# Wider groups and longer lags in the gather stage of a graph layer with experts

## The chip, the cores and the metric

The kernel runs on one core of one Trainium2 chip. The metric is device time in microseconds (us) of one execution. TensorE is written PE, VectorE DVE, ScalarE ACT, GpSimd POOL, SyncE SP; SP issues most of the direct DMAs, POOL issues the gathers.

## The reference, cut to what matters

`x` has 12500 nodes of 256 numbers. There are 212500 edges `src -> dst`, sorted by `dst`; every node has an edge to itself among them (a self-loop), which comes last among the edges of its node.

```python
h   = x * rsqrt(deg_out)[:, None]
m   = segment_sum(h[src], dst) * rsqrt(deg_in)[:, None]
y0  = m @ W_gc + b_gc + x @ W_res + b_res
y   = y0 + moe(y0)              # top 2 of 64 experts, 256 -> 512 -> 256
out = layernorm(x + batchnorm(y) * gamma + beta)
```

## The kernel before, in words

The kernel has five stages, one after another.

**Degrees** (L257 to L434). The out-degrees are counted with one-hot matrices in PE, and `r_out`, their inverse root, is made. In between, `columns` (L268) loads the edges of the head groups (below) and `windows` (L282) makes `n0`, the first node of each group's window.

**Scaled rows and the check** (L516 to L598). `x` lies in `acc` as 14 sets of columns. DVE (L533) and ACT (L531) scale them by `r_out`; SP stores each set to `h_d` in DRAM (L535). `Lanes.fetch` (L456) loads the edges of the lane groups, `src` and `dst`, into the tile `room`: pass 0 has 128 lanes, pass 1 has 54, of which the last is loaded by a DMA of its own (L467). `fitting` (L491) counts on DVE what does not fit in the windows; its steps are dealt out between the scalings (L538 to L541). Then `acc` is set to zero in 14 parts (L553, ten on POOL and four on DVE), each as soon as the store of that set has landed. A block under `If(unfit > 0)` (L557) is skipped when everything fits; no instruction moves across it.

**Gather rows** (L600 to L1119). A row is 128 edges: POOL gathers 128 rows of `h_d` by `src_col` into one of six `ring` buffers of four rows (L683), and PE multiplies them with a one-hot matrix `o` made by DVE (`one_hot`, L671), adding up a group of `GR = 8` rows in PSUM (L696). A group spans a window of `W = 128` nodes. There are `NG = 198` groups, so 1584 rows. The first `HG = 16` (head) groups take edges as they come. The other 182 take `L = 1078` edges each, of which `SKIP = 54` self-loops are left out and the remaining 1024 fill 8 rows; the self-loops are added from the window's own rows of `h_d` (`own`, L709, a DMA of SP; `add_own`, L738). To leave them out, `compact` (L990) runs 40 DVE steps over 1078 columns, once for the lanes of pass 0 and once for pass 1: compare, mark, a running count, then six rounds (`BITS`) of four operations that shift the kept edges together. `lay` (L1044), `lay_turn`, `laid` transpose the result into `src_col` and `rel`, and `marks` (L1074) takes a flag apart. The lanes lie in the last columns of `acc`, which are first saved to `lent_d` (L601) and later loaded back (L1108); the second `Lanes.fetch` (L603) loads them there, and its three memsets are on DVE (L462, L470).

After a group: `out_of` (ACT copy of PSUM, L730), `add_own` and `numbers` (DVE), `turn` (two PE transposes, L766), `to_nodes` (DVE adds into `acc` and into the in-degrees, L793). When all edges of a tile of 128 nodes are in, `nodes` (L816) works on a pair of tiles: in-degree root, `scale` of `x` (ACT), `turn_x` (PE), `dense` (PE, `y0` and the expert logits), `best` (DVE, top 2), `count` and `ranks` (position within each expert), `codes`, and for each tile and choice `entries` (DVE) and `enter` (PE), which write into `tab`, two tables in PSUM (tile number and lane) that say which node sits in which expert slot. `dense` to `best` and `count` to `ranks` take the two tiles of a pair one after the other, since `gp` and `pp` are in one PSUM bank.

The order is written out by hand (`tc.manual_schedule`, L1101): on PE, DVE, ACT and POOL each instruction of the stage comes in the order in which the program gives it. The loop (L1111) gives one `row(c)`, one `one_hot(c + AHEAD)`, and then those steps of the heap `todo` whose time, counted in rows, has come. A step gives its successor a time `lag` rows later (`later`, L641): 6 rows, falling to 1 towards the end. Instructions that stand outside that block, such as `Lanes.fetch`, are put by the compiler among them.

**End of the rows** (L1122 to L1182). `tab` is turned into a list of nodes (`slot`), and the experts are ordered by size.

**Experts and normalisation** (L1185 on). For each expert gather, two layers, scatter; then batch and layer norm.

Of the kernel before, what the change touches and what calls it, by code (L numbers as in the profile page):

```python
# [43 lines left out]
GR = 8  # L44
NG = 198
HG = 16
# [3 lines left out]
L = -(-(M - HE) // NL)  # L50
# [11 lines left out]
def center(g):  # L62
    return (241 * g) >> 2 if g < HG else CEN + ((2029 * (g - HG)) >> 5)

# [35 lines left out]
def gnn_moe_kernel(  # L100
# [26 lines left out]
    lent_d = dram.tile([P, 5 * L + 2 * ((L + 2) // 2)], F32, name="lent_d")  # L127
# [114 lines left out]
    n0_lane = edge.tile([P, 2], F32)  # L242
# [4 lines left out]
    with ExitStack() as stack:  # L247
# [20 lines left out]
        def columns():  # L268
            g = tables.rearrange("p a b c -> p (a b c)")[:, : 2 * P].rearrange(
                "p (k c) -> p k c", c=P  # L270
            )
            for k, e in enumerate((src, dst)):
                nc.sync.dma_start(g[:, k], e[:HE].rearrange("(p c) -> p c", c=P))
            f = two.tile([P, 4, P], F32, name="col_f")
            S.copy(f[:, :2], g)
            p = ps2.tile([P, 4, P], F32, name="col_p")
            for k in range(2):
                T.transpose(p[:, k], f[:, k], ident)
            S.copy(src_col[:, :HC], p[:, 0])
            S.copy(rel[:, :HC], p[:, 1])  # L280

        def windows():  # L282
# [10 lines left out]
            GP.iota(cen[:, :HG], pattern=[[241, HG]], base=0, channel_multiplier=0)  # L293
            GP.iota(cen[:, HG:], pattern=[[2029, NL]], base=CEN << 5, channel_multiplier=0)
            V.tensor_single_scalar(cen[:, :HG], cen[:, :HG], 2, op=ALU.arith_shift_right)
# [27 lines left out]
            for k, (lim_of, op) in enumerate(((0.0, ALU.is_lt), (float(W), ALU.is_ge))):  # L323
                V.tensor_scalar(
                    junk[:, k], rel[:, :HC], lim_of, None, op0=op, op1=ALU.add,
                    accum_out=bad[:, k : k + 1],
                )
# [110 lines left out]
    count = [P, NL - P]  # L438
    HALF = (L + 2) // 2
    ROOM = 5 * L + 2 * HALF  # L440

    class Lanes:
        def __init__(self, room):
            self.given = [
                [room[:, (2 * k + i) * L : (2 * k + i + 1) * L].bitcast(I32) for i in range(2)]
                for k in range(2)
            ]
            self.buf = room[:, 4 * L : 5 * L]

            self.left = room[:, 5 * L : 5 * L + HALF].bitcast(BF16)[:, : L + 1]  # L450
            self.at = room[:, 5 * L + HALF :].bitcast(BF16)[:, :L]
            self.is_self, self.again = (
                self.buf.bitcast(BF16)[:, i * L : (i + 1) * L] for i in range(2)
            )

        def fetch(self):  # L456
            for k in range(2):
                for i, e in enumerate((src, dst)):
                    t = self.given[k][i]
                    n = count[k] - k  # L460
                    if k:
                        V.memset(t, (0, BEHIND)[i])  # L462
                    a = HE + k * P * L
                    b = a + n * L
                    nc.sync.dma_start(t[:n], e[a:b].rearrange("(p c) -> p c", c=L))
                    if k:
                        nc.sync.dma_start(  # L467
                            t[n : n + 1, : M - b], e[b:].rearrange("(p c) -> p c", p=1)
                        )
            V.memset(self.left, 0.0)  # L470

        def leave_out(self, k, n_left):

            r = count[k]
            s, d = (t[:r] for t in self.given[k])
# [10 lines left out]
                    self.at[:r], d, n0_lane[:r, k : k + 1], 255.0,  # L486
# [4 lines left out]
    def fitting(lanes, k, n_left):  # L491

        r = count[k]

        def outside(i, lim_of, op):
            V.tensor_scalar(
                lanes.is_self[:r], lanes.at[:r], lim_of, None, op0=op, op1=ALU.add,
                accum_out=bad[:r, 2 + 2 * k + i : 3 + 2 * k + i],
            )

        def begins():
            junk = lanes.buf[:r, :r]
            V.scalar_tensor_tensor(
                junk, n0_b[:r, 0, HG + k * P : HG + k * P + r], 1.0, ident[:r, :r],
                op0=ALU.mult, op1=ALU.mult, accum_out=n0_lane[:r, k : k + 1],
            )

        return [begins] + lanes.leave_out(k, n_left) + [
# [3 lines left out]
                bad[:r, 6 + k : 7 + k], n_left[:r], SKIP - 0.5, op=ALU.is_lt  # L512
# [3 lines left out]
    with ExitStack() as stack:  # L516
# [5 lines left out]
        n_left = one.tile([P, 2], F32, name="n_left")  # L522
        steps_of = []
        for k in range(2):
            steps_of += fitting(lanes, k, n_left[:, k : k + 1])
        for i, (t0, n) in enumerate(GROUPS + [(NT - 1, 1)]):
# [11 lines left out]
            if i > 1:  # L538
                for f in steps_of[:2]:
                    f()  # L540
                del steps_of[:2]  # L541
        for f in steps_of:
# [63 lines left out]
    with ExitStack() as stack:  # L606
# [5 lines left out]
        hp = inner.enter_context(tc.tile_pool(name="s_hot", bufs=3))  # L612
# [11 lines left out]
        zero = one.tile([P, 2 * D], F32)  # L624
# [5 lines left out]
        tab = [ps1.tile([P, NSLOT], F32, name=f"tab{k}") for k in range(2)]  # L630

        bank = ps1.tile([P, 4 * P], F32, name="bank")
        gp = bank[:, :DL]
        pp = bank[:, DL : DL + 2 * E].rearrange("p (k e) -> p k e", e=E)
# [3 lines left out]
        LAG = 6  # L638
        todo = []

        def later(t, f, k=1):  # L641
            lag = min(LAG, max(1, LAG + (NC - 100 - t) // 10))
# [24 lines left out]

        o_of, o_last, row_last = {}, {}, {}
        p_of, s_of = {}, {}

        def one_hot(c):  # L671
            g, j = divmod(c, GR)
            if j == 0:
                o_of[g] = hp.tile([P, GR, W], F32, name="o")
            o_last[g] = V.tensor_scalar(  # L675
                o_of[g][:, j], lane, rel[:, c : c + 1], None, op0=ALU.is_equal
            )

        def row(c):
# [16 lines left out]
            i = T.matmul(p_of[g], o_of[g][:, j], r[:, k], start=j == 0, stop=j == GR - 1)  # L696
            if j == 0:
                sync(i, o_last.pop(g))
            if k == RR - 1:
                row_last[u] = i  # L700
            if j == GR - 1:
                del o_of[g]
                later(c, lambda t: out_of(g, t))

        spare = tables.rearrange("p a b c -> p (a b c)").bitcast(F32)
# [3 lines left out]
        def own(g):  # L709
# [3 lines left out]
            if g % 4 == 0:  # L713
                n = min(4, NG - g)
# [8 lines left out]
            nc.sync.dma_start(own_of[g], h_d[bass.ds(own_begins["n0"][g % 4], W)])  # L723


        def out_of(g, t):
# [8 lines left out]
            else:  # L735
                later(t, lambda t: turn(g, s, None, t))

        def add_own(g, s, t):  # L738
# [5 lines left out]
            if g % 2 == 0:  # L744
                later(t, lambda t: turn(g, s, None, t))

        def numbers(g, s, t):
            add_own(g, s, t)
            shift = two.tile([P, 2, P], F32, name="shift")
# [11 lines left out]
            later(t, lambda t: turn(g, s, (shift, e), t))  # L761
# [16 lines left out]
        def to_nodes(g, q, t):  # L778
# [15 lines left out]
            if g % 2 == 0:  # L794
                return
            k = first_node(g - 1) // P
            V.tensor_add(deg_in[:, k : k + TD], q[:, 2 * P : 2 * P + TD], deg_in[:, k : k + TD])
            ready = first_node(g + 1) // P if g < NG - 1 else NT
            while begun[0] < NT:
# [3 lines left out]
                nodes(begun[0], n, t)  # L803
                begun[0] += n

        xts = {}

        def fetch(t0):
# [3 lines left out]
            xts[t0] = two.tile([P, 2, D], F32, name="xt")  # L812
# [3 lines left out]
        def nodes(t0, n, t):  # L816
# [28 lines left out]
            def scale(t):  # L845
                for i in range(n):
                    S.activation(xt[:r, i], xt[:r, i], AF.Copy, scale=v["root"][:r, i : i + 1])
                later(t, turn_x)
# [11 lines left out]
            def turned(t):  # L860
                q = v.pop("q").rearrange("p (i k n) -> p i k n", i=2, k=2)
                S.copy(of("xT", [P, 2, 2, P])[:, :n, :, :r], q[:, :n, :, :r])
                of("y", [P, 2, DL])
                of("top", [P, 2, 8])
                of("i8", [P, 2, 8], U32)
                take("gp", t, lambda t: dense(0, t))

            def dense(i, t):
                a = (t0 + i) * P
                for k in range(2):  # L870
                    T.matmul(gp[:r], acc2[:, k, a : a + r], wcat[:, k], start=k == 0, stop=False)  # L871
                for k in range(2):
                    T.matmul(  # L873
                        gp[:r], v["xT"][:, i, k, :r], wcat[:, 2 + k], start=False, stop=k == 1
                    )
                later(t, lambda t: best(i, t))

            def best(i, t):
                y, top, i8 = v["y"], v["top"], v["i8"]
                V.scalar_tensor_tensor(  # L880
                    y[:r, i], gp[:r], r_in[:r, t0 + i : t0 + i + 1], bias[:r],
                    op0=ALU.mult, op1=ALU.add,
                )
                V.max(top[:r, i], y[:r, i, D:])
                V.max_index(i8[:r, i], top[:r, i], y[:r, i, D:])
                if i < n - 1:
                    later(t, lambda t: dense(i + 1, t))
                    return
                give("gp", t)
                nc.sync.dma_start(  # L890
# [18 lines left out]
                take("pp", t, lambda t: count(0, t))  # L909
# [8 lines left out]
            def count(i, t):  # L918
                both = v["both"]
                T.matmul(pp[:r, 0], before[:r, :r], both[:r, i], start=True, stop=True)  # L920
                T.matmul(pp[:, 1], ones_b[:r], both[:r, i], start=True, stop=True)  # L921
                later(t, lambda t: ranks(i, t))

            def ranks(i, t):
                ahead = of("ahead", [P, E])
# [583 lines left out]
```

## Time and profile before

| what | us |
|---|---|
| median of 10 runs (lowest, highest) | 3413.92 (3411.93, 3418.39) |
| the profiled execution | 3413.97 |
| its span, first to last instruction | 3412.0 |
| `r_out` ready, first lane load issued | 196.65 |
| first gather of the rows starts | 258.64 |
| last gather of the rows starts | 2286.88 |
| first gather of the experts starts | 2325.45 |

| engine | busy us | share |
|---|---|---|
| PE | 2662.3 | 78% |
| DVE | 1753.8 | 51% |
| ACT | 748.3 | 22% |
| POOL | 2035.4 | 60% |

Times in the trace are counted from the first instruction. The profile names instructions by line, engine, operation and tiles; "SPq" is the queue of DMAs that SP issues. A wait is put down to what ended it; "issue" is time in which nothing that the profile shows was waited for.

### The profile page before, as it was taken

To read this page: it belongs to the slowest core of one execution; us is meant where nothing else is said; L and a number is where in the kernel's file an instruction comes from. 1 tells how busy PE (TensorE), PEld (TensorE's weight loads), DVE (VectorE), ACT (ScalarE), POOL (GpSimd) and SP (SyncE) were. 2 spreads that over 40 slices of the span, in tenths; PEclk is the share of its full clock that TensorE was granted. 3 is DMA by queue.
4 is the path that set the end of the run, shared out by engine and by line. 5 is a ranking of instruction groups with operands and counts; after the bars stand their busy time and mean duration, and the time that the engine had idled before them with its cause. 6 is when DMAs were issued, how large, how long until landed. Compare 5 with 4: busy or idle time off the path is not lost. (4 is left out here: it accounts for less than half of the span.)

```text
span 3412.0 us, 38328 instructions
## 1 busy us (share of the span) xinstructions
PE 2662.3 (78%) x11391; PEld 1774.1 (52%) x11391; DVE 1753.8 (51%) x6362; ACT 748.3 (22%) x2080; POOL 2035.4 (60%) x2086
## 2 busy tenths in 40 slices
PE   6723777777777777778777877877999999999644
PEld 5613444444444444444444444554778766778533
DVE  9977354855555555555555555574222221222498
ACT  8840010111111111111111111111222211222368
POOL 0017777777777777777777777764555555554100
PEclk8766888788988888988989889988999999999765
DMA  5058744354444444444444444434344445556667
GB/s 173 2 172 299 260 130 125 112 168 128 131 128 131 132 131 131 130 130 129 129 131 130 129 133 131 130 116 124 118 124 134 126 152 163 177 182 197 221 214 239
DMA packets 264826, 506.70 MB, mean 149 GB/s; under 512 B 45451, under 2 KB 177977, under 8 KB 256166
## 3 DMA queue, kind: packets, MB, share of 16 engines
q0 software_dynamic: 98800, 264.95, 26.7%
q1 hardware_dynamic: 152516, 226.44, 20.2%
q10 hardware_dynamic: 13298, 12.80, 1.3%
q8 instruction: 93, 1.52, 0.2%
q14 instruction: 119, 0.97, 0.1%
HBM read 411.01 MB, written 96.44 MB: 149 GB/s over the span
## 5 line engine op out<-in xcount | busy, mean ns | idle before, releaser
L683 POOL DMA_INDIRECT ring<-h_d,src_col x1584 | 1546.9, 977 | 494.2 <-issue 421.6
L696 PE MATMUL p<-ring,o 128*128 128x258 f32 x3168 | 1141.8, 466 | 485.0 <-DMA ring<-h_d,src_col 367.1
L696 PEld LDWEIGHTS p<-ring,o 128*128 128x128 f32 x3168 | 571.2, 212 | 950.0 <-DMA ring<-h_d,src_col 693.6
L675 DVE TENSOR_SCALAR o<-lane,rel 128x128 f32<-128x128 f32 x1584 | 394.4, 298 | 167.3 <-PE p L696 167.2
L1249 PE MATMUL yp<-w,h 128*128 128x256 f32 (+3 forms) x1928 | 432.9, 380 | 0.0
L1205 POOL DMA_INDIRECT xg<-x_d,tables x241 | 232.9, 967 | 317.8 <-PE xtp L1220 219.0
L730 ACT COPY s<-p 128x258 f32<-128x258 f32 x198 | 74.0, 374 | 1511.1 <-PE p L696 1489.8
L1233 PE MATMUL hp<-xT,w 128*128 128x384 f32 (+11 forms) x1328 | 399.2, 454 | 1.4 <-DVE xT L1224 1.4
L1249 PEld LDWEIGHTS yp<-w,h 128*128 128x128 f32 (+3 forms) x1928 | 341.8, 182 | 64.5 <-issue 7.3
L1237 ACT ACTIVATE h<-hp,w 128x384 f32<-128x384 f32 (+11 forms) x332 | 180.9, 545 | 669.8 <-PE hp L1233 669.3
L1233 PEld LDWEIGHTS hp<-xT,w 128*128 128x128 f32 x1328 | 248.4, 191 | 131.1 <-issue 56.7
L1255 POOL DMA_INDIRECT z_d<-yo,tables x241 | 238.1, 988 | 121.9 <-DVE yo L1254 65.3
L1224 DVE COPY xT<-xtp 128x768 f32<-128x768 f32 (+2 forms) x83 | 77.3, 932 | 405.1 <-PE xtp L1220 405.1
L880 DVE SCALAR_TENSOR_TENSOR y<-bank,r_in,bias 128x320 f32<-128x320 f32 x98 | 53.9, 550 | 378.0 <-PE bank L921 271.5
L1254 DVE TENSOR_TENSOR yo<-yp,bb 128x256 f32<-128x256 f32 (+3 forms) x241 | 102.0, 423 | 276.4 <-PE yp L1249 272.4
L793 DVE TENSOR_TENSOR acc<-q,acc 128x256 f32 x198 | 83.1, 420 | 226.9 <-PE q L770 114.3
L405 ACT ACTIVATE s_lo<-lane_b,nb 128x128 bf16<-128x128 bf16 x581 | 170.8, 390 | 3.7 <-DVE lo_end L396 2.5
L871 PE MATMUL bank<-wcat,acc 128*128 128x320 f32 x392 | 157.3, 535 | 1.3 <-DVE total L927 0.7
L553 POOL MEMSET acc<- 128x1792 f32 x10 | 15.9, 1591 | 228.6 <-DMA h_d<-acc 227.8
L982 PE MATMUL tab<-at,vals 128*128 128x512 bf16 x392 | 124.2, 402 | 10.3 <-DVE vals L971 10.2
L873 PE MATMUL bank<-wcat,xT 128*128 128x320 f32 x392 | 132.1, 462 | 0.0
L871 PEld LDWEIGHTS bank<-wcat,acc 128*128 128x128 f32 x392 | 96.0, 246 | 37.0 <-issue 14.7
(279 smaller groups left out, 2744.5 us busy)
## 6 DMA issues: line engine op xcount, KB each, us to landing
w<-in_wpack SPq DMA_DIRECT2D x64, 1026.0 KB, 5.3
ring<-h_d,src_col POOLq DMA_INDIRECT x1584
z_d<-zero SPq DMA_DIRECT2D x98, 256.0 KB, 5.2
zt<-z_d SPq DMA_DIRECT2D x24, 1024.0 KB, 7.1
tables<-h_d SPq DMA_DIRECT2D x182, 128.0 KB, 2.3
xt<-in_x ACTq DMA_DIRECT2D x48, 256.0 KB, 3.1
x_d<-y SPq DMA_DIRECT2D x48, 256.0 KB, 2.4
z<-in_x SPq DMA_DIRECT2D x12, 1024.0 KB, 7.3
```

The costliest lines, as they stand in the source:

```text
L405: S.activation(s_lo[:, i], lane_b, AF.Sign, bias=nb[:, k, i : i + 1])
L675: o_last[g] = V.tensor_scalar(o_of[g][:, j], lane, rel[:, c : c + 1], None, op0=ALU.is_equal)
L683: i = GP.indirect_dma_start(out=r[:, k, :D], out_offset=None, in_=h_d, in_offset=bass.IndirectOffsetOnAxis(ap=src_col[:, c : c + 1], axis=0),)
L696: i = T.matmul(p_of[g], o_of[g][:, j], r[:, k], start=j == 0, stop=j == GR - 1)
L871: T.matmul(gp[:r], acc2[:, k, a : a + r], wcat[:, k], start=k == 0, stop=False)
L873: T.matmul(gp[:r], v["xT"][:, i, k, :r], wcat[:, 2 + k], start=False, stop=k == 1)
L982: T.matmul(tab[m], vals[:r, m], at[:r], start=t0 + i + k == 0, stop=t0 + i == NT - 1 and k == 1,)
L1205: GP.indirect_dma_start(out=g, out_offset=None, in_=x2_d, in_offset=bass.IndirectOffsetOnAxis(ap=at[:, 0, k : k + 1], axis=0),)
L1233: T.matmul(hp[:, :m], w1[:, c, j * P : (j + 1) * P], xT[:, c, :m], start=c == 0, stop=c == 1,)
L1237: S.activation(h1[:, j, :m], hp[:, :m], AF.Gelu, bias=w[:, 2 * H + 4 * D + j : 2 * H + 4 * D + j + 1],)
L1249: T.matmul(yp[:r], h1[:, j, k * P : k * P + r], w2[:, j], start=j == 0, stop=j == 3,)
L1255: st = GP.indirect_dma_start(out=z_d, out_offset=bass.IndirectOffsetOnAxis(ap=at[:r, 1, k : k + 1], axis=0), in_=yo[:r], in_offset=None, b ...
```

## The change

Groups have twelve rows, and there are 132 of them, so again 1584 rows. The head has 14 groups (168 rows). The other 118 fit in one pass of 118 lanes with `L = 1620` edges, of which 84 self-loops are left out; seven rounds in `compact`. The second pass is gone, two copies to float are added at its end in place of the ACT copies of `lay`. The steps of the pass are spread over the first 101 rows. `Lanes.fetch` sets all lanes to zero first, on POOL, and `fitting` comes after all scalings. The lag is 11 rows instead of 6. One-hot matrices come in units of six rows, five buffers, 16 rows ahead. `dense` to `best` and `count` to `ranks` take both tiles of a pair at once (a second PSUM bank); the two tables become one, in which both numbers are summed. A counter (`hold`) lets at most two transposes be under way. Where several units of tiles become ready at once, each starts six rows after the one before.

```diff
-GR = 8
-NG = 198
-HG = 16
+GR = 12
+NG = 132
+HG = 14
...
-L = -(-(M - HE) // NL)
+L = -(-(M - HE) // NL // 2) * 2
...
         def fetch(self):
-            for k in range(2):
-                for i, e in enumerate((src, dst)):
-                    t = self.given[k][i]
-                    n = count[k] - k
-                    if k:
-                        V.memset(t, (0, BEHIND)[i])
...
-            V.memset(self.left, 0.0)
+            b = HE + (NL - 1) * L
+            for i, e in enumerate((src, dst)):
+                t = self.given[i]
+                GP.memset(t, (0, BEHIND)[i])
+                nc.sync.dma_start(t[: NL - 1], e[HE:b].rearrange("(p c) -> p c", c=L))
+                nc.sync.dma_start(
+                    t[NL - 1 : NL, : M - b], e[b:].rearrange("(p c) -> p c", p=1)
+                )
+            GP.memset(self.left, 0.0)
...
-            if i > 1:
-                for f in steps_of[:2]:
-                    f()
-                del steps_of[:2]
-        for f in steps_of:
+        for f in fitting(lanes, n_left):
             f()
...
-        hp = inner.enter_context(tc.tile_pool(name="s_hot", bufs=3))
+        hp = inner.enter_context(tc.tile_pool(name="s_hot", bufs=5))
...
-        tab = [ps1.tile([P, NSLOT], F32, name=f"tab{k}") for k in range(2)]
-
-        bank = ps1.tile([P, 4 * P], F32, name="bank")
-        gp = bank[:, :DL]
-        pp = bank[:, DL : DL + 2 * E].rearrange("p (k e) -> p k e", e=E)
-        LAG = 6
+        tab = ps1.tile([P, NSLOT], F32, name="tab")
+        banks = [ps1.tile([P, 4 * P], F32, name=f"bank{i}") for i in range(2)]
+        gps = [b[:, :DL] for b in banks]
+        pps = [b[:, DL : DL + 2 * E].rearrange("p (k e) -> p k e", e=E) for b in banks]
+        LAG = 11
...
-            lag = min(LAG, max(1, LAG + (NC - 100 - t) // 10))
+            lag = min(LAG, max(1, (NC - 10 - t) // 12))
...
+        def hold(t, f):
+            to_turn.append(f)
+            next_turn(t)
+
+        def next_turn(t):
+            while to_turn and turning[0] < 2:
+                turning[0] += 1
+                to_turn.pop(0)(t)
...
             ready = first_node(g + 1) // P if g < NG - 1 else NT
+            wait = 0
             while begun[0] < NT:
                 n = 2 if begun[0] < NT - 2 else 1
                 if begun[0] + n > ready:
                     break
-                nodes(begun[0], n, t)
+                if wait:
+                    at_row(t + wait, lambda t, t0=begun[0], n=n: nodes(t0, n, t))
+                else:
+                    nodes(begun[0], n, t)
                 begun[0] += n
+                wait += 6
...
-                        tab[m], vals[:r, m], at[:r],
+                        tab, vals[:r, m], at[:r],
...
+                lambda: V.tensor_copy(before_[:, full], m[:, full]),
+                lambda: V.tensor_copy(f[:, full], b[:, full]),
...
-        def compact_from(k, c):
-
-            per = 1 if k else 0.5
-            steps_of = compact(k)
...
+        def compact_by(c):
+
+            steps_of = compact()
+            lays = [(j, which) for j in range(0, GR, 4) for which in range(2)]
+            c -= 3 * len(lays) + 3 * LAG
+            for i, f in enumerate(steps_of):
+                at_row(c * i / len(steps_of), lambda t, f=f: f())
...
-            AHEAD = GR + 2
+            AHEAD = 16
             fetch(0)
-            compact_from(0, 0)
-            c = compact_from(1, 2 * P)
+            compact_by(HC - AHEAD)
...
-        V.scalar_tensor_tensor(node, node, float(P), tab[1], op0=ALU.mult, op1=ALU.add)
```

## The prediction

> **What bounds the kernel now.** I read the slices of the page first, then its costliest group, then the waits of POOL.
>
> ```profile
> PE   6723777777777777778777877877999999999644
> DVE  9977354855555555555555555574222221222498
> POOL 0017777777777777777777777764555555554100
> ...
> L683 POOL DMA_INDIRECT ring<-h_d,src_col x1584 | 1546.9, 977 | 494.2 <-issue 421.6
> ```
> ```profile
> POOL ring L683 <- issue: 421.6, 1384, 0.3
> ...
> POOL ring L683 <- PE p L696: 28.6, 94, 0.3
> ```
>
> POOL stands at 7 through the rows, and its gathers never wait: no idle time before one is longer than 0.4 us except the first. A gather takes 0.945 us undisturbed plus 0.30 between two: 1.25 us, and windows of 100 us hold 80 of them all the way. 1584 x 1.25 = 1980 us, but the rows last from 258.64 to 2287.83, that is 2029: some 50 us of gathers that are themselves longer. PE (78% busy) waits for the gathers, not they for it. So what can move the time is when the rows begin, what stretches a gather, and what follows the last one. Lag, units of one-hots, pairs at once and the counter of transposes change when PE, DVE and ACT do things that POOL does not wait for: nothing within the rows, with 24 ring rows (30 us) of cover; without it a late row costs its lateness. The row count stays 1584.
>
> **(a) Before the rows.** Windows of the DMAs between `r_out` and the first row:
>
> ```profile
> 201.00:206.00 5.00, 0.00 (x0) 0.00 (x0) 5.00 (x6) 5.00 (x13) 0.00 (x0) 0.50 0.08 30
> 206.00:213.00 7.00, 0.00 (x0) 0.00 (x0) 7.00 (x8) 4.16 (x11) 0.00 (x0) 0.50 0.91 306
> 213.00:220.00 7.00, 0.00 (x0) 0.00 (x0) 2.96 (x4) 0.00 (x0) 0.00 (x0) 0.50 0.07 26
> 221.00:252.00 31.00, 0.19 (x2) 0.11 (x2) 20.46 (x24) 0.00 (x0) 15.91 (x10) 0.50 1.01 341
> ```
>
> The last two columns are DMA share and GB/s. Twice the DMAs run at 26 GB/s, a sixteenth: one engine of 16, busy with the two 223 KB loads of 53 lanes. First SP sits 6.29 us in the load issued at 199.13; then a `fitting` step on DVE waits 4.8 us for such a load and the scalings behind it come late (SP waits 7.4 us for DVE). In between and after, the stores run at 341 GB/s. About 13 us are lost. After: no 53-lane load, and scalings ahead of all `fitting` steps. DVE then has 9 sets of 2.02 us done by about 215, faster than the stores take them; `fitting` (ten steps, some 12 us at 1620 columns) ends by 230, before the stores. Against it, the first load now waits for a POOL memset: 1.59 us for 1792 columns (L553), so 1.44 for 1620. The loads are 117 x 1620 x 4 B = 758 KB each. Is that shape fast? The 128-lane one (539 KB) landed in 4.8 us; by that row 6.8 us, by the 53-lane one 29 us on one engine. I take the 128-lane row, the nearer. **-12 us**, ends -14 and (one engine) +32. The Trainium skill ("DMA: Bandwidth & Descriptors", "Why a DMA increments its semaphore by 16 and not by 1") says that a DMA uses the largest number up to 16 that divides its outer sizes; that agrees with 53 on one engine, and would give 117 thirteen, leaving the sum as it is.
>
> **(b) Memsets in POOL's queue.** The second fetch, after the `If`, has three memsets on POOL that must wait until the copy to `lent_d` has read its columns; the gathers stand behind them. That copy was issued at 257.74 and DVE's memset got through at 268.85: 11.1 us. How many gathers the compiler puts ahead of the memsets is not in this trace, but SP's order is: three of the 98 zero stores came ahead of the loads that wait for the same copy, so I take four gathers (5 us). POOL then idles 11.1 - 0.9 - 5 = 5.2 us, and the memsets take 3 x 1.44 plus gaps: **+10 us**. Ends: 4.3 (nine gathers or more ahead), 14.5 (none). The first gather is seen 0.9 us after that copy's issue. The lanes then land about 20 us after the rows begin; 16 one-hots are made by then.
>
> **(c) What stretches gathers.** The order of DVE and POOL during pass 0:
>
> ```profile
> 284.68 2.40 DVE L998 TENSOR_TENSOR_SCAN acc<-acc 128x1078 f32<-128x1078 bf16 x1
> 285.00 2.84 POOL L683 DMA_INDIRECT ring<-h_d,src_col  x1 [0.30 <-issue]
> ...
> 296.31 1.27 DVE L1026 TENSOR_TENSOR acc<-acc 128x1078 int32<-128x1078 int32 x1
> 296.62 1.78 POOL L683 DMA_INDIRECT ring<-h_d,src_col  x1 [0.30 <-issue]
> 297.62 1.28 DVE L1027 TENSOR_TENSOR acc<-acc 128x1078 int32<-128x1078 int32 x1
> 298.70 1.01 POOL L683 DMA_INDIRECT ring<-h_d,src_col  x1 [0.30 <-issue]
> ```
>
> A gather that starts while DVE runs a long operation on two SBUF tiles goes on only at that operation's end and then takes 0.83 us: 297.58 + 0.83 = 298.41, seen 298.40. So do the others of this pass. An operation that begins more than 0.1 us after the gather does not hurt it, and the DVE operations themselves do not stretch (L1026: 1.261 to 1.275 us). Summed over 0.945 us, pass 0 costs 12 us and pass 1 14 us. They are that cheap because DVE is full: operations of 1.27 us, end to end, each catch at most one gather late in its run.
>
> After: 46 steps at 1620 columns, one per 2.2 rows. There are 29 two-input steps of 1.27 x 1620 / 1078 = 1.91 us. A gather starts somewhere in each; on average half a period (0.63) after its beginning, and 0.1 is free: 1.91 - 0.73 = 1.18 us, 34 us in all. The scan (2.40, so 3.6) gives 2.9. The 14 short ones (0.72, so 1.07 us, seen to hold a gather too) catch one only part of the time: 0.97 x 0.97 / 2.5 = 0.37 each, 5. Together 42 instead of 26: **+16 us**. Ends: 0 in all (-26), and 1.8 for each of the 29 (+34). DVE has room: 75 us of steps and 25 of one-hots in 101 rows, 126 us and more. If it had none, the layout at row 101 would be late; it is needed at row 152. The Trainium skill ("SBUF — State Buffer", "Who interferes with whom") says that DVE and POOL share one pair of ports and that whichever issues first blocks the other. As an estimate by that rule, were half of the collisions to fall on DVE, this part would cost 21 and the time would be 3420; in this trace the gather is the one that waits.
>
> **(d) Steady rows.** `add_own` (0.476 us, two SBUF tiles, x182) stretches gathers by 0.04 us on average in the windows I summed; 64 fewer: **-3 us**. `to_nodes` reads PSUM and stretched none. The phase to POOL's beat may change; at worst each of 118 loses 0.3 us more, +35, at best -8.
>
> **(e) After the last gather.** Its start is R, now 2286.88.
>
> ```profile
> 2286.88 0.95 POOL L683 DMA_INDIRECT ring<-h_d,src_col  x1 [0.30 <-issue]
> 2325.45 0.94 POOL L1205 DMA_INDIRECT xg<-x_d,tables  x1 [37.63 <-DVEq L1293]
> ```
>
> By `first_node` the last group now sets free tiles 96 and 97, both at once, step by step side by side; the pair 94 was under way before. After, with 95 nodes per group, it sets free 94+95, 96 and 97, six steps apart. At lag 1 that is an order in which `dense` of 96 stands on PE behind the last `enter` of 94, and `scales` of 97 on DVE behind `best` of 96. From the rows of this tail: gather to PE 2.8, matmul 0.7, copy, `numbers`, `turn`, `to_nodes` to R + 6.9 (now R + 11.3, behind pair 94). Pair 94: root and `scales` 1.7, `scale` to `xT` 2.6, `dense` 3.7 + 2.4 (first tile on a slow clock), `best` 3.1: R + 20.5. `scales` 96 1.2, `ranks` 2.0, `codes` 1.25, `entries` 4 x 0.65, to 27.5; PE's four `enter` of 0.95 end at 29.4. `dense` 96 2.5, `best` 2.0: 33.9. `scales` 97, `ranks`, `codes`, `entries`: 38.6; `enter` 39.8; `dense` 97 2.5, `best` 2.0: 44.3; `ranks` to `enter`: 49.3. Slot list 5.25, less 0.75 for the second table: 53.8; copies and first gather: R + 55.1. Now it is R + 38.6: **+16.5 us**. Ends: +8 (DVE's work of a pair, 12 us, less the 4.4 of the earlier start) and +20.
>
> The rest is covered: what `columns` adds is one short memset against smaller `windows`; 66 fewer own loads are SP's; ACT is 22% busy.
>
> **Sum.** -12 + 10 + 16 - 3 + 16.5 = +27.5. The profiled execution took 3413.97 (span 3412.0, 2.0 around it), 0.05 over the median of the runs. Forecast 3441.
>
> **Rivals.** *Gathers go free* (faster): with steps spread out, DVE comes upon a gather already under way and waits for it. For it: DVE is no longer full, and gathers fill 76% of POOL's time. Against it: DVE's unchanged durations. Waits of (c) at zero: 27.5 - 42 = -14.5, 3399; below 14 us of waits in all, it turns the sign. *Light*: memsets without idle (+5), tail at +9, (c) at 30: 3413 to 3420. *Heavy*: add_own and entries fall on POOL's beat: up to 3475. *One engine for 117 lanes*: two loads of 29 us in a row, +32 in (a) and about +30 at the second fetch: 3490 to 3505; against it, the shape is nearer to 128. *The change does not do what it says*: the slow path under `If`. Counted on the reference's own edges, no edge falls outside a window and the poorest lane has 87 self-loops for 84: left out.
>
> **Chances.** Forecast (3424 to 3456) 0.64, light 0.14, gathers free 0.10, heavy 0.07, one engine 0.05. A change of 0.2% is about what a measurement here can tell (3407.1 and 3420.7): light lies within it for 0.11. So faster 0.10, same 0.11, slower 0.79. The range 3414 to 3460 leaves out the free gathers, one engine and the edges of light and heavy.
>
> **What would show it.** (a) first gather near 246 and no 26 GB/s windows; (b) three POOL memsets among the first gathers, with idle time ahead; (c) gathers of 1.5 to 2.9 us spread over the first 100, none later; (e) R to the experts' first gather near 55 us. I am wrong if DVE's long steps stretch instead of gathers, or if the tail's units overlap.

## The result, and the profile after

| what | before | after |
|---|---|---|
| median of the runs shown with the result, us | 3414.43 (28 runs) | 3429.75 (8 runs, 3427.11 to 3431.81) |
| ratio | | 1.0044 [1.0035, 1.0052] |
| span of the profiled execution | 3412.0 | 3424.9 |
| first gather of the rows starts | 258.64 | 243.74 |
| last gather of the rows starts | 2286.88 | 2284.79 |
| first gather of the experts starts | 2325.45 | 2339.59 |
| gathers above 0.945 us, summed over all rows | 52.5 | 60.4 |

The changed kernel is slower by 0.4%. The profiled execution after took 3426.7 us, 3.0 below its median; the account below is of the spans, which differ by 12.9. The last row of the table, and every "excess" below, is added up from durations as the views print them, to 0.01 us; from the unrounded records it is 51.0 and 58.8, with nearly the same difference.

The page of the changed kernel: three lines of the slices, and its costliest group.

```profile
PE   6824777777777778777777777776999999999644
...
DVE  9976434454445445445454455664222222222498
...
POOL 0038777777777777777777777754555555554100
...
L693 POOL DMA_INDIRECT ring<-h_d,src_col x1584 | 1554.8, 982 | 495.2 <-issue 425.4
```

POOL's third slice reads 3 and read 1, its fourth 8 and 7: the rows now begin within the third (part of that 3 is memsets that have moved to POOL). The 1584 gathers (now L693) take 982 ns on average and took 977. The waits of POOL in front of them (sum, times, longest):

```profile
POOL ring L693 <- issue: 425.4, 1397, 0.3
...
POOL ring L693 <- PE p L707: 43.9, 144, 0.3
```

As before none of these is above 0.3 us: POOL sets the pace. In all the rows two gaps are longer than 0.4 us, one with the three memsets (below) and one of 1.2 us at row 140, which a DMA of the ring ended. Then the stretches between `r_out` (195.3) and the first row, with DMA share and GB/s last:

```profile
199.00:205.00 6.00, 0.00 (x0) 0.00 (x0) 6.00 (x5) 6.00 (x17) 0.77 (x1) 0.50 0.94 299
205.00:232.00 27.00, 0.19 (x2) 0.11 (x2) 19.66 (x21) 3.98 (x10) 15.93 (x10) 0.50 1.06 365
```

The DMA engines are nearly full from 199 to 232; nothing moves at 26 GB/s any more. At the second fetch, POOL's order of time:

```profile
272.80 0.94 POOL L693 DMA_INDIRECT ring<-h_d,src_col  x1 [0.30 <-issue]
273.73 2.86 POOL L461 MEMSET acc<- 128x1620 int32 x2
276.50 1.48 POOL L466 MEMSET acc<- 128x1621 bf16 x1
278.15 0.95 POOL L693 DMA_INDIRECT ring<-h_d,src_col  x1 [0.16 <-issue]
```

The three memsets stand behind 24 gathers. The gather after them would have begun at 274.05, so they cost 4.1 us, with no idle time ahead of them. The compaction, DVE beside POOL:

```profile
314.78 1.84 DVE L1051 TENSOR_TENSOR acc<-acc 118x1620 int32<-118x1620 int32 x1
314.90 2.54 POOL L693 DMA_INDIRECT ring<-h_d,src_col  x1 [0.30 <-issue]
...
316.54 0.67 DVE L685 TENSOR_SCALAR o<-lane,rel 128x128 f32<-128x128 f32 x3
317.12 1.84 DVE L1052 TENSOR_TENSOR acc<-acc 118x1620 int32<-118x1620 int32 x1
317.74 2.04 POOL L693 DMA_INDIRECT ring<-h_d,src_col  x1 [0.31 <-issue]
```

The step of 314.78 ends at 316.62; 0.83 us later, at 317.45, the gather that started on it is seen to end at 317.44. The same holds at 317.12: 318.96 + 0.83 = 319.79, seen 319.78. The DVE steps do not stretch (1.84 us each). Last, the end of the rows on POOL and PE:

```profile
2284.79 0.95 POOL L693 DMA_INDIRECT ring<-h_d,src_col  x1 [0.30 <-issue]
2339.59 0.94 POOL L1222 DMA_INDIRECT xg<-x_d,tables  x1 [53.85 <-DVE tables L1319]
```
```profile
2309.23 3.44 PE L1007 MATMUL tab<-at,vals 128*128 128x512 bf16 x8 [2.45 <-DVE vals L996]
2312.50 1.24 PE L893 MATMUL bank<-wcat,acc 128*128 128x320 f32 x4
...
2320.64 1.89 PE L1007 MATMUL tab<-at,vals 128*128 128x512 bf16 x4 [1.84 <-DVE vals L996]
2322.32 2.34 PE L893 MATMUL bank<-wcat,acc 128*84 128x320 f32 x4
```

L1007 is `enter`, L893 `dense`. `dense` of tile 96 (2312.50) comes right behind the last `enter` of pair 94, and `dense` of tile 97 (2322.32) right behind that of tile 96: the three units run one after the other. From the last row's gather to the first expert's it is 54.8 us, and was 38.6.

### The profile page after: what moved, and what is told of

It is laid out like the page before. It is cut to its first block, busy times and chain, and to the rows that moved or that the text cites. A ratio compares the mean times of both kernels' runs of the same rounds, so it can differ in the third digit from the quotient of the medians.

```text
span 3424.9 us, 37022 instructions
## 1 busy us (share of the span) xinstructions
PE 2663.8 (78%) x11121; PEld 1764.4 (52%) x11121; DVE 1635.7 (48%) x6013; ACT 707.8 (21%) x1994; POOL 2051.8 (60%) x2092
## 5 line engine op out<-in xcount | busy, mean ns | idle before, releaser
L693 POOL DMA_INDIRECT ring<-h_d,src_col x1584 | 1554.8, 982 | 495.2 <-issue 425.4
L707 PE MATMUL p<-ring,o 128*128 128x258 f32 x3168 | 1184.1, 484 | 506.8 <-DMA ring<-h_d,src_col 411.4
L707 PEld LDWEIGHTS p<-ring,o 128*128 128x128 f32 x3168 | 611.6, 224 | 998.5 <-DMA ring<-h_d,src_col 652.2
L685 DVE TENSOR_SCALAR o<-lane,rel 128x128 f32<-128x128 f32 x1584 | 375.5, 298 | 607.2 <-PE p L707 607.0
L742 ACT COPY s<-p 128x258 f32<-128x258 f32 x132 | 49.4, 374 | 1300.9 <-PE p L707 1298.5
L1007 PE MATMUL tab<-at,vals 128*128 128x512 bf16 x392 | 141.4, 451 | 11.3 <-DVE vals L996 11.3
L893 PE MATMUL bank<-wcat,acc 128*128 128x320 f32 x392 | 133.2, 466 | 0.0
L806 DVE TENSOR_TENSOR acc<-q,acc 128x256 f32 x132 | 55.6, 422 | 146.4 <-PE q L783 103.8
L898 PE MATMUL bank<-wcat,xT 128*128 128x320 f32 x392 | 123.9, 439 | 0.0
L702 ACT CAST ring<-mark 128x4 f32<-128x4 bf16 x354 | 57.8, 197 | 261.3 <-issue 261.2
L414 PE MATMUL deg_s<-o_hi,s_lo 128*128 128x98 bf16 x581 | 76.8, 232 | 27.5 <-DVE o_hi L202 18.3
```

The lines of the kernel that those rows point to most:

```text
L685: o_last[u] = V.tensor_scalar(o_of[u][:, j], lane, rel[:, c : c + 1], None, op0=ALU.is_equal)
L693: i = GP.indirect_dma_start(out=r[:, k, :D], out_offset=None, in_=h_d, in_offset=bass.IndirectOffsetOnAxis(ap=src_col[:, c : c + 1], axis=0),)
L707: i = T.matmul(p_of[g], o_of[v][:, n], r[:, k], start=j == 0, stop=j == GR - 1)
L893: T.matmul(gps[i][:r], acc2[:, k, a : a + r], wcat[:, k], start=k == 0, stop=False,)
L898: T.matmul(gps[i][:r], v["xT"][:, i, k, :r], wcat[:, 2 + k], start=False, stop=k == 1,)
L1007: T.matmul(tab, vals[:r, m], at[:r], start=t0 + i + k + m == 0, stop=t0 + i == NT - 1 and k + m == 2,)
```

## The experiments

They ran on other chips, three of them, which granted TensorE a lower clock: 0.787 over the changed kernel's span where the first chip gave 0.857. The kernel before took 3700 to 3706 us there. Times are compared only on the same chip, and the kernel before ran on each; for the rest the parts of the spans are compared. "Excess" is the sum of what gathers took above 0.945 us.

### The changed kernel on such a chip

> The changed kernel itself, as the measure for the others of this call on their chip. If this chip grants PE a clock of about 0.86, as in the profile after: ratio to the kernel before 1.0044 (1.0035 to 1.0052), excess of the gathers over 0.945 us in rows 0 to 95 45 us, in the others 15 us, 54.8 us from the start of the last row's gather to that of the first expert's. Where the clock is nearer to 0.79, PE sets the pace of the rows and what stretches gathers counts for less: ratio about 1.00, while excess and end of the rows stay what they are (within 3 us).

3714.96 us, ratio 1.0034 [1.0020, 1.0049]; excess 45.0 in rows 0 to 95 and 17.1 in the others; end of the rows 60.3. One line of the windows of each, first the changed kernel on the first chip, then here:

```profile
1200.00:1300.00 100.00, 76.28 (x253) 44.76 (x254) 46.51 (x222) 9.61 (x40) 75.93 (x80) 0.86 0.44 127
```
```profile
1200.00:1300.00 100.00, 65.62 (x218) 43.67 (x216) 39.40 (x195) 7.33 (x31) 66.34 (x70) 0.73 0.38 111
```

The third figure from the right is the granted clock. 80 gathers in 100 us became 70, and the waits of POOL say why:

```profile
POOL ring L693 <- issue: 437.1, 1424, 1.2
...
POOL ring L693 <- remote: 164.3, 61, 4.1
...
POOL ring L693 <- PE p L707: 102.9, 57, 8.5
```

Where the view says "remote", the profile names no instruction that ended the wait. But apart from the three memsets POOL stands still for more than 0.4 us in front of 107 gathers, and 104 of these are the first of a ring buffer: it waits for PE to free the ring, up to 8.5 us at a time, which it never did on the first chip. PE sets the pace. What stretches a gather is the same in both (45.0 us), but part of it is hidden behind PE; the end of the rows is longer, because PE lags behind the last gather: its last product of a row ends 10.2 us after that gather starts, and 5.1 on the first chip. The ratio near 1.00 that was expected for such a clock was too low: the end of the rows and the first rows still count.

### The compaction in pieces

```diff
+            def each(f, a=0, z=L):
+                k = 4
+                n = -(-(z - a) // k // 2) * 2
+                for x in range(a, z, n):
+                    out_steps.append(lambda x=x, y=min(x + n, z): f(x, y))
...
-                    lambda: V.tensor_tensor(b, w, m, op=ALU.bitwise_and),
+                each(lambda x, y: V.tensor_tensor(
+                    b[:, x:y], w[:, x:y], m[:, x:y], op=ALU.bitwise_and))
```

So for every step but the scan and a memset. A sum in `leave_out` (`n_left`) that nothing reads there is left out.

> The changed kernel with each step of the compaction (but the scan and one memset) cut into four pieces of about 405 columns. Theory (a gather that starts under a long two-input operation waits for that operation's end, so the price grows with the square of its length): the first 96 gathers lose some 12 us over 0.945 us each instead of 45, first to last gather about 2008 us, time about 3397. Rival (a price per operation, or per microsecond of DVE work): four times as many operations and as much work, so the gathers lose 45 us or more, time 3430 or above.

Excess in rows 0 to 95 24.7 us (45.0 in again, 45.7 in wait2); rows 152 on are unchanged. Time 3697.5, ratio 0.9984 [0.9973, 0.9995]. So the price is one of length and not of number, and the rival falls. But 24.7 is twice what was expected; the run `chain` shows why.

### The units of tiles closer together

```diff
-                wait += 6
+                wait += 2
```

> The changed kernel with the units of tiles that become ready together started two rows apart instead of six; that happens only after the last group. Theory (the order puts one unit's steps behind another's): last gather of the rows to first gather of the experts about 44 us instead of 54.8, time about 3419. Rival (the added pair of tiles costs its own work, whatever the order): 50 us or more, time 3425 or above.

3704.93, ratio 1.0004 [0.9994, 1.0014]. The end of the rows on POOL:

```profile
2561.55 0.95 POOL L693 DMA_INDIRECT ring<-h_d,src_col  x1 [0.30 <-issue]
2610.30 0.94 POOL L1222 DMA_INDIRECT xg<-x_d,tables  x1 [47.80 <-DVE tables L1319]
```

48.75 us, against 59.3 and 60.6 in the two other runs on this chip that have the changed kernel's end (split4 and dvemem): 10.5 to 11.9 less, 10.8 expected. The rival falls. The kernel before takes 51.3 us for this stretch here (in loads48, below), so on this chip the end lost 8 to 9 us and not 16, and the six rows between the units are more than all of it. On the first chip 11 of the 16 would be most of it; that was not run.

### The memsets on DVE

```diff
-                GP.memset(t, (0, BEHIND)[i])
+                V.memset(t, (0, BEHIND)[i])
...
-            GP.memset(self.left, 0.0)
+            V.memset(self.left, 0.0)
```

> The changed kernel with the three memsets of each lane fetch back on DVE. Theory (they cost the gathers exactly their own 4.1 us in POOL's queue, nothing else): first to last gather 2037 instead of 2041, the lanes land about 20 us sooner, time about 3426. Rival (what matters is when the lanes land, and DVE's wait for the copy takes its place): no change, 3429 to 3431, or later rows.

3712.02, ratio 1.0025 [1.0014, 1.0037]. First to last gather of the rows 2310.5 us, against 2314.4 to 2315.5 with the memsets on POOL: 3.9 to 5.0 less, as the theory has it. The first gather came 1.4 us later than in wait2: the first fetch's memsets now stand on DVE ahead of the scalings, which begin 5.1 us after `r_out` where they began at once.

### The kernel before with its 53-lane loads cut

```diff
-                    nc.sync.dma_start(t[:n], e[a:b].rearrange("(p c) -> p c", c=L))
+                    for p0, p1 in ((0, n),) if n == P else ((0, 48), (48, n)):
+                        nc.sync.dma_start(
+                            t[p0:p1],
+                            e[a + p0 * L : a + p1 * L].rearrange("(p c) -> p c", c=L),
+                        )
```

> The kernel before with each load of 53 lanes issued as one of 48 and one of 5; the checks stay dealt out between the scalings. Theory (the 53-lane loads run on one DMA engine and hold up the stores): no stretch at 26 GB/s, first gather near 246 instead of 258.6, time about 3401. Rival (the dealing out of the checks holds up the stores): first gather at 254 or later, time 3410 or above.

3688.72, ratio 0.9967 [0.9954, 0.9981]. Its windows at the place of the 30 and 26 GB/s:

```profile
201.00:206.00 5.00, 0.00 (x0) 0.00 (x0) 5.00 (x6) 5.00 (x14) 0.00 (x0) 0.50 1.04 283
206.00:213.00 7.00, 0.00 (x0) 0.00 (x0) 7.00 (x6) 4.04 (x11) 3.41 (x3) 0.50 1.05 346
213.00:221.00 8.00, 0.00 (x0) 0.00 (x0) 8.00 (x13) 0.00 (x0) 5.51 (x4) 0.50 1.06 359
```

The first gather starts at 245.18, with `fitting` still between the scalings. From the end of `r_out` to it are 48.8 us, and 62.2 in the kernel before (on the first chip): 13.3 less. The time is 14.0 us less than the kernel before's on this chip. The two loads on one engine account for it, the order of the checks does not (the rival falls).

### Another lag

```diff
-        LAG = 11
+        LAG = 6
```

> A lag of 6 rows in place of 11, nothing else. My theory: the lag moves when PE, DVE and ACT do a group's steps, which POOL does not wait for; that the rows outside the compaction lost 10 us of excess and not 3 comes from there being 118 lane groups and not 182 (fewer add_own, numbers, copies). So 0, ratio to the changed kernel within 0.1%; excess of rows 96 to 1583 stays at 15 us, the end of the rows at 55 us. Rival, the phase: with the lag of before the steps fall on POOL's beat as before, excess of rows 96 to 1583 goes to 22 us or more, and the time is 7 us longer. Second rival, the lag is a cover for PE: rows wait for PE and the time grows by over 10 us.

3708.87 (3706.56 to 3713.02) against 3714.96, so 6 us less where 0 was expected; the intervals of the two ratios (1.0013 to 1.0033 and 1.0020 to 1.0049) overlap. Excess of rows 96 on 17.3 us, 4.0 of it in rows 96 to 143, since the compaction's steps now reach there; without those 13.3, and 16.7 in again. The first rival wanted 22 or more and falls, and the second was a loss. Rows 152 on took 2063.0 us and 2068.4 in again: the gain lies where PE sets the pace.

### The compaction's steps closer together

```diff
-                at_row(c * i / len(steps_of), lambda t, f=f: f())
+                at_row(0.7 * c * i / len(steps_of), lambda t, f=f: f())
```

> The 46 compaction steps are given out over 71 rows in place of 101, nothing else. My theory: a gather waits for what remains of the step of DVE on which it starts, and goes on 0.83 us after that step's end; with steps end to end the next gather starts 0.83 + 0.30 = 1.13 us after a step's end, so 1.13 us into the next one of 1.91 us, and loses 0.78 us, where with gaps it loses 1.18 us on the average. So the 29 long steps cost about 29 x 0.78 = 23 us and not 34: excess of rows 0 to 95 35 us and not 45, the time shorter by 10 us (where POOL sets the pace). Rival: each step costs the same wherever it stands; excess stays at 45 us, the time the same. Second rival: DVE has too little room, one-hots come late and the rows wait for them; the time longer by 5 us or more.

3715.89, the same; excess in rows 0 to 95 41.1, 3.9 less and not 10. The steps were as close as they get: DVE stood still for 0.4 of the 85 us in which they ran, and for 31 of 125 us in again. The 28 bit steps (the seven rounds of four) caught 22 gathers for 25.0 us here and 22 for 27.0 in again. So a step costs nearly the same whether the next is near or far, and the reason given in (c) for the cheapness of the kernel before, that its DVE was full, is at most a small part of it: the rival is the nearer. Row 152 starts at the same time (246.1 us after the first) in both: the 3.9 us were lost again to waits for the ring, which grew by 4.0 us up to there.

### Three costs out at once

The pieces, `wait += 2`, and `fetch` with the engine of its memsets as an argument (POOL the first time, DVE the second).

> Three of the costs taken out at once: compaction steps (but for the scan) in four pieces, units of tiles two rows after one another and not six, and the second fetch's memsets on DVE (the first fetch's stay on POOL, whose move cost 1.4 us). My theory: the gains add up, since they lie in different stretches: 21 us in rows 0 to 95 as the run of the pieces alone showed (45.7 to 24.7), 11 us at the end, 4 us at the memsets; 36 us below the changed kernel, ratio to the kernel before 0.994 where POOL sets the pace of the rows. Where PE does (clock near 0.79), the first of them counts for little and 15 to 20 us stay. Rival: what is gained on POOL is lost to the next bound (PE) in the same stretch on any chip, and only the 11 us at the end stay: ratio 1.001.

3679.89, ratio 0.9951 [0.9935, 0.9968], 35.1 below again: 36 was expected where the gains add up. Excess of rows 0 to 95 25.9, end of the rows 48.75, rows 152 on 2064.8. That the first counts for little under a low clock was wrong. That the gains add up is only in part what the profiles show. The end gave 11.6 us. By row 152 best is 19.1 us ahead of again, where 25 were expected: 19.1 of excess and 4.1 of memsets went, and 4.0 of waits for the ring came. The other 8.4 of the 39.1 us between the two spans (an earlier first gather 2.1, the later rows 3.6, the experts 2.8) lie where none of the three edits acts, so the match with 36 is partly luck.

### The pieces in another order

This is `best` with the bit steps ordered by piece:

```diff
-            for i in range(BITS):
-                by = 1 << i
-                each(lambda x, y, i=i: V.tensor_scalar(
...
+            for i in range(BITS + 1):
+                for x, y in parts:
...
+                        out_steps.append(lambda x=x, y=y: V.tensor_tensor(
+                            b[:, x:y], w[:, x:y], m[:, x:y], op=ALU.bitwise_and))
+                        out_steps.append(lambda x=x, y=y: V.tensor_tensor(
+                            w[:, x:y], w[:, x:y], b[:, x:y], op=ALU.bitwise_xor))
```

> The kernel best with the pieces of the bit steps in another order: all steps of one piece after one another, so that each needs the result of the one before it. In best the four pieces of one step follow one another, need nothing of each other, and run with an overlap of 0.08 us: no gap between them, and gathers there were caught by two pieces in a row (7 gathers above 1.6 us in the bit steps, 15.3 us of excess). Theory: a gather goes on at the first gap, and 0.04 us between two steps that depend on each other is enough, so each gather is caught by one piece of about 0.57 us (two at the few places where a piece follows an independent one): excess in the bit steps 15.3 to about 9 us, at most 2 gathers above 1.6 us, all rows 0 to 95 from 25.9 to 20 us. Rival: a gather needs a longer gap or a one-hot between; excess in the bit steps stays at 15 us. Time: 0 to 6 us below best, by how much POOL sets the pace of these rows.

First pieces of one step in a row, in `best`, then a piece of `chain` (the POOL line is the gather):

```profile
287.21 2.05 POOL L693 DMA_INDIRECT ring<-h_d,src_col  x1 [0.30 <-issue]
287.38 1.06 DVE L1049 SCALAR_TENSOR_TENSOR acc<-acc 118x406 f32<-118x406 bf16 x2
```
```profile
323.45 0.57 DVE L1069 TENSOR_TENSOR acc<-acc 118x406 int32<-118x406 int32 x1
323.47 1.36 POOL L693 DMA_INDIRECT ring<-h_d,src_col  x1 [0.30 <-issue]
```

In `best` two pieces run as one of 1.06 us (x2): the gather goes on only at 288.44, the end of the second, and ends at 289.26. In `chain` it goes on after one, at 324.02; a one-hot follows there (323.94 to 324.22), and it does not hold the gather. Excess of the bit steps 15.3 to 5.6 us, longest gather there 2.07 to 1.37, none above 1.6 (7 before); rows 0 to 95 13.3 us, which is about the 12 that split4 was expected to give. So the doubling there was pieces without a gap. That 0.04 us between two steps are enough is seen in the kernel before too: in the prediction's lines L1026 ends at 297.58, L1027, which needs its result, begins at 297.62, and the gather went on between them. Time 3677.72, ratio 0.9930 [0.9913, 0.9946], against 0.9951 for `best` on another chip, where the intervals overlap: the gain in time is not shown, the fall of the excess is.

### The shorter lag once more

> The kernel best with a lag of 6 rows in place of 11. In the changed kernel this gave -6 us (3708.9 against 3715.0) where 0 was expected, 2 us of it less excess in rows 0 to 143 and 3 to 5 us in the later rows. Theory: a shorter lag lets PE's matmuls of the rows and the other steps mix better where PE sets the pace (granted clock near 0.79); so again 4 to 6 us below best there, and 0 to 1 us where the clock is nearer to 0.86 and POOL sets the pace. Rival: those 6 us came with the clock of those runs and not with the lag; no difference to best.

3677.1, ratio 0.9923 [0.9907, 0.9940]. Excess of rows 0 to 143 falls by 5.1 us (26.3 to 21.2), rows 152 on take 2067.2 (2064.8 in `best`): no gain where lag6 had its own. It ran on another chip than `best`, and the two intervals overlap.

> The kernel chain with a lag of 6 rows in place of 11, so that the compaction's steps are given out over 116 rows and not 101. Theory: what a shorter lag gave (6 us in the changed kernel, 0 to 3 in best) is only the sparser compaction, since in best the later rows did not gain; chain has 13 us of excess left there, so at most 2 us go, and the time stays within 3 us of chain. Rival: the lag helps PE in the later rows; 5 us less. If the granted clock is near 0.86 here, POOL sets the pace and all gains on POOL count: about 3380 us, ratio to the kernel before 0.990; near 0.79, about 3675, ratio 0.993.

3673.45, ratio 0.9913 [0.9896, 0.9931], 4.3 below `chain` on the same chip, the lowest of all. Excess of rows 0 to 143 15.1 (14.7 in `chain`), rows 152 on 2066.8 (2070.1). The kernel before took 2.7 us less too in the executions beside chain6 than in those beside `chain`. The lag of 6 came out shorter in three pairs (1.0034 to 1.0023, 0.9951 to 0.9923, 0.9930 to 0.9913), each time with another part of the span to show for it, and in each pair the intervals overlap. The direction is the same thrice; neither the gain nor its cause is settled.

## Why the prediction was right

It said slower, 3441 with 3414 to 3460; the median is 3429.75. The sum in its own terms:

| step | forecast | measured | from |
|---|---|---|---|
| (a) before the rows | -12 | -14.9 | 258.64 to 243.74 |
| (b) memsets on POOL | +10 | +4.1 | 274.05 to 278.15 |
| (c) compaction stretches gathers | +16 | +16.9 | 28.1 to 45.0 |
| (d) steady rows | -3 | -9.0 | 24.4 to 15.4 |
| (e) end of the rows | +16.5 | +16.2 | 38.6 to 54.8 |
| rest of the rows, the experts | 0 | -0.4 | +0.8, -1.2 |
| sum | +27.5 | +12.9 | spans |

(c) is the excess of rows 0 to 95, and before of the second pass too (rows 248 to 303); (d) is that of the other rows. By the unrounded records they are +17.3 and -9.5, so the split between them is good to half a microsecond.

**(a)** The mechanism holds and is shown from the other side: the kernel before gains 13.3 us up to its first gather when its 53-lane loads alone are cut. The 117-lane loads are not one-engine loads (299 GB/s right behind them). 1.2 us of the 14.9 are an earlier `r_out`, which was not forecast. The Trainium skill ("DMA: Bandwidth & Descriptors", "Why a DMA increments its semaphore by 16 and not by 1") has a DMA use the largest number up to 16 that divides its outer sizes: 53 gives one, 48 gives sixteen. The rates agree: 26 GB/s before, 283 to 359 in loads48. (The prediction set 758 KB, in thousands of bytes, beside 539 and 223, in units of 1024 bytes; with one unit its 6.8 us are 6.6, and nothing hangs on it.)

**(b)** This step was mis-sized. The part that failed is "so I take four gathers": there were 24, so POOL did not idle 5.2 us, and only the memsets' own 4.1 us stayed, which was the lower bound (4.3). The order of another queue, SP's, was the wrong row to read the compiler's order on POOL from.

**(c)** Right in size and in the rule for a gather that starts on a step: each of the 21 two-input bit steps caught one gather, for 26.6 us in all, 1.27 each where 1.18 was reckoned, and the scan cost 2.5 (2.9). The pieces (24.7 us, then 13.3 when ordered by dependence) show that the length of the uninterrupted DVE work is the price. What does not hold is the reason given for the kernel before being cheap: in `dense` crowded steps cost almost as much. By the runs with pieces the length of its steps (1.27 us and not 1.84) is the likelier part; no run of the kernel before varied it. Gathers did not go free: the `bitwise_and` of L1051 took 1.84 us with a gather waiting behind it and not more. By the Trainium skill ("SBUF — State Buffer", "Who interferes with whom") whichever issues first blocks the other. Here no 1.84 us step before which a gather had started took longer (28 in six profiles, at most 1.85 us), so the collisions did not fall on DVE by half and the 21 us of that estimate were not seen. Only pieces that began within 0.02 us of a gather were longer, 0.61 us in the middle of 19 against 0.57.

**(d)** The larger of the two misses. Fewer `add_own` was right, but not the whole. Between 900 and 2200 us, a gather started on 74 of 129 `add_own` before (9.3 us of excess) and on 16 of 86 after (2.4 us); counted is a start from 0.1 us before the step's start to 0.1 us before its end. By their number alone 9.3 would have become 6.2, the 3 us of the forecast. The rest is where they fall on POOL's beat: the prediction named that phase as an unknown and took it as neutral. That it fell well is luck. On the other chips the difference is not there: 40 of 112 in loads48 (5.7 us) and 27 of 76 in again (5.0 us), a third each. So the number of groups alone does not make it. Whether the lag does is open: lag6 has 23 of 76 and 2.3 us, half of again, but no run on the first chip has the changed kernel with a lag of 6.

**(e)** Right in each place: pair 94 to `best` R + 20.5 (seen 19.6), the last `enter` of it 29.4 (27.9), `enter` of tile 96 39.8 (37.7), first expert 55.1 (54.8). And wait2 takes 10.5 to 11.9 back.

The 14.6 us between forecast and measured span are (b) 5.9 and (d) 6.0 and (a) 2.9 less (c) 0.9, with 0.7 of small terms. The median lies in the forecast's own band (3424 to 3456); none of the rivals came: no load on one engine, no free gathers, memsets without idle as in the light case but with an end of the rows at its full price, and `add_own` off POOL's beat where the heavy case had it on. The two misses, (b) and (d), lie on the same side, so the sum is not right by one error hiding another: the change is slower by about half of what was forecast.

The forecast also rested on 24 ring rows as a cover for PE. At a clock of 0.857 that held. At 0.787 POOL waits for PE, as the changed kernel does in again and the kernel before in loads48 (110 waits above 0.4 us), and there the change still cost 0.3%.

## What to carry to other kernels

Find out which engine's instruction is stretched by another before dealing out work: long two-input DVE steps beside gathers cost a gather the rest of the step, so cut them into pieces, and order the pieces so that each needs the one before it; 45 us of excess became 13 here. A spacing that is meant to keep units apart (six rows between tiles) is paid in full at the end of the loop, where nothing is left to fill it: there 11 us. Read the shape of each load in a busy queue: two of 53 partitions ahead of 14 stores cost 13 us.

## What the runs showed of the hardware

- A two-input DVE step that does not depend on the one before begins 0.08 us before that one's end (in `best` 286.20 + 0.57 = 286.77, the next at 286.69). Counted over the compaction's steps in all thirteen profiles: a gather held by the first of two such steps went on only at the second's end in 57 of 74 cases, and at the first's end in 17; what sets these apart was not settled. Where 0.03 to 0.04 us lay between the steps, because the second needs the first's result, it went on at the first's end in 17 of 17 (16 of them in the kernel before and loads48). The Trainium skill ("VectorE: DVE Perf Modes", "The DRAIN you can't avoid") says that the next operation starts when the pipe is empty, unless it is not held; the start after the end and the start before it are both seen here, the pipe is in no view.
- When a gather can still be caught by a step that begins after it was not settled. The prediction had up to 0.1 us. Counted are gathers at whose start no two-input step ran, and steps of more than 0.5 us. Where the step began within 0.13 us of the gather's start, 49 of 57 took at most 1.01 us. Of the seven with 0.15 to 0.18 us, four were held (2.05, 2.04, 2.05 and 1.55 us). From 0.2 us on, 69 of 85 took less than 1.05 us.
- Both kernels ran 8% longer on three other chips (the kernel before 3414 and 3700 to 3706 us). In the same window of the rows the changed kernel's granted clock was 0.86 and 0.73, and the engine that bounds the rows changed with it. Whether it is the chip or what else ran there, no run separates.
- On every chip the changed kernel's granted clock is below the kernel before's: 0.857 and 0.875 in the two profiles on the first, 0.785 to 0.793 and 0.806 to 0.817 in the runs beside again. No run shows why.
